# 3x3 convolutions on TensorE: minimal filtering along rows alone, against minimal filtering along rows and columns with 1 MB filter pieces

## Chip, cores, metric

One core of one Trainium2 chip, everything in float32. The metric is the device time of one execution in microseconds (us). A time given for a kernel is the median of its runs.

## The reference

Eight images of 512 channels x 32 x 32, group norm, then a block with two bottlenecks; each bottleneck has a 3x3 convolution over 256 channels followed by attention over all 1024 positions with four heads.

```python
t = cbs(x, cv1_w, cv1_bn, 0)                  # 1x1 convolution, batch norm, silu: 512 -> 512
ys = [t[:, :C], t[:, C:]]                     # C = 256
for i in range(2):
    yi = ys[-1]
    z = cbs(yi, m_cv1_w[i], m_cv1_bn[i], 1)   # the 3x3 convolution, 256 -> 256
    z = bot_attention(z, m_qkv_w[i], m_rw[i], m_rh[i])
    z = silu(bn_eval(conv2d(z, m_cv2_w[i], 0), m_cv2_bn[i]))
    ys.append(yi + z)
out = x + cbs(concatenate(ys, axis=1), cv2_w, cv2_bn, 0)
```

## The kernel before

A 3x3 convolution with output rows in tiles of four needs, for each output, fewer multiplications if rows are combined first: F(4,3) makes six combinations of six input rows, multiplies each by a combination of the filter's rows, and combines the six results into four rows. The three taps along a row remain ordinary taps. The stages are: combine filters once (first image, then kept in DRAM), combine input rows on VectorE, multiply on TensorE, combine result rows on VectorE, then silu.

```python
def make_u(n, oc, k):                          # filters, first image only
    ...
    nc.vector.tensor_tensor(even, g0, g2, ALU.add)
    nc.vector.scalar_tensor_tensor(u[:, 1], even, -4.0, odd, ALU.mult, ALU.add)
    ...                                        # 6 operations on VectorE, 3 on ScalarE
    nc.gpsimd.dma_start(u_dram[n][oc][k], u)

def conv3x3(n, vs, u_of):
    z = act.tile([P, NM, HW], F32, tag="z", name="z")
    for oc in range(NM):                       # NM = 2 blocks of 128 channels
        us = [u_of(oc, k) for k in range(NM)]
        mid = ps_big.tile([P, 4, NT * F], F32, tag="big", name="c3_mid")
        ...                                    # end: the two outer combinations
        for pos in (1, 2, 3, 4, 0, 5):         # row combinations
            dst = mid[:, pos - 1, :] if 0 < pos < 5 else end[:, pos // 5, :]
            for i in range(NM * 3):            # input block and tap
                k, dx = divmod(i, 3)
                nc.tensor.matmul(
                    dst, us[k][:, pos, dx, :], vs[k][:, pos, :, dx : dx + F],
                    start=(i == 0), stop=(i == NM * 3 - 1),
                )
        rows_out(z[:, oc, :], mid, end)        # VectorE, reads PSUM
        k = bn_m1[n] + oc
        for half in range(NH):
            part = z[:, oc, ts(half, HALF)]
            t = act.tile([P, HALF], F32, tag="t", name="t", bufs=2)
            nc.scalar.activation(t, part, AF.Tanh, scale=sh[:, k : k + 1], bias=bh[:, k : k + 1])
            nc.vector.tensor_scalar(
                part, part, sh[:, k : k + 1], bh[:, k : k + 1], ALU.mult, ALU.add
            )
            nc.vector.scalar_tensor_tensor(part, t, 1.0, part, ALU.add, ALU.mult)
    return z
```

`rows_in` (VectorE, per input block: three operations over 512 elements and six over 256) makes the row combinations `v_in`. After a convolution come the 1x1 projections to q, k and v. The first few of them need only the first block of 128 channels, and TensorE does those while the second block's output and activation are still under way. "Tail" below is the time from the start of the last convolution matmul to the first projection matmul that needs the second block.

## Time and profile before

Median 2671.78 us (2671.65 to 2671.93). The chain of waits and the groups are shown in the prediction. In the views, PE is TensorE's matmuls, PEld its weight loads, DVE VectorE, ACT ScalarE, POOL GpSimd and SP SyncE; L254 is a line of the kernel in question.

### The profile page before, as it was taken

The page shows a single profiled execution, that of the slowest core. Times are in us where ns is not written, and L with a number is a line of the kernel's source. Part 1 is how long each engine was busy: PE and PEld are TensorE (multiplying, and loading weights), DVE is VectorE, ACT ScalarE, POOL GpSimd, SP SyncE. Part 2 cuts the span into 40 slices and gives each one's busy share as a digit, 9 for nine tenths or more (in the row PEclk, how much of TensorE's full clock was granted, in tenths as well). Part 3 has the DMA queues.
Part 4 walks back from the last instruction along what each step waited for, and adds up shares of the span by engine and source line. Part 5 has one row for each costly group of instructions (what it writes and reads, how often), then busy time and mean ns, then how long its engine had stood idle before and what let it go on. Part 6 is the DMA issues. An engine that isn't in the chain of part 4 may idle for free.

```text
span 2669.4 us, 33857 instructions
## 1 busy us (share of the span) xinstructions
PE 2582.2 (97%) x13858; PEld 1300.7 (49%) x13858; DVE 1397.0 (52%) x2036; ACT 989.4 (37%) x1337; POOL 103.5 (4%) x246
## 2 busy tenths in 40 slices
PE   6999999999999999999999999999999999999898
PEld 3536355363553635446364453635536354363633
DVE  5565645645356453564636546265552645536453
ACT  2342523524234241443414434153431534315252
POOL 2000010000100001000010000100000000000000
PEclk9999999999999999999999999999999999999999
DMA  6113021030310203112031110402104011130001
GB/s 227 52 67 116 14 99 70 14 117 14 110 61 25 103 14 132 40 53 74 14 132 41 58 68 14 165 12 74 52 27 150 10 54 41 40 138 14 32 14 57
DMA packets 81571, 174.08 MB, mean 65 GB/s; under 512 B 31872, under 2 KB 41600, under 8 KB 73216
## 3 DMA queue, kind: packets, MB, share of 16 engines
q1 hardware_dynamic: 69664, 129.33, 14.2%
q0 software_dynamic: 11744, 42.51, 4.7%
q8 instruction: 111, 1.82, 0.3%
q14 instruction: 52, 0.43, 0.0%
HBM read 144.87 MB, written 26.94 MB: 64 GB/s over the span
## 4 chain that ended last, share of the span: by engine, by line
PE 86%; issue 4%; DVE 4%; ACT 3%; DMA 1%; SPq 0%; DVEq 0%; ACTq 0%
PE ps L254 33%; PE av_ps L458 14%; PE l_ps L435 13%; PE c_mid L625 12%; PE c_end L625 6%; PE v_ps L401 4%; ACT pt L439 3%; PE s_ps L475 2%; PE m_ps L647 2%; DVE acc L444 1%; DVE ao L466 1%; DVE st L325 1%; DMA rs<-r_dram 0%; DVE acc L442 0%; ACT h L240 0%
## 5 line engine op out<-in xcount | busy, mean ns | idle before, releaser
L439 ACT ACTIVATE pt<-l_ps 128x1024 f32<-128x1024 f32 x512 | 496.3, 1026 | 236.2 <-PE l_ps L435 230.4
L444 DVE TENSOR_TENSOR acc<-acc,pt 128x1024 f32<-128x1024 f32 x384 | 469.6, 1223 | 147.3 <-ACT pt L439 122.9
L458 PE MATMUL av_ps<-pt,vT 64*64 64x512 f32 x4096 | 492.9, 597 | 9.9 <-DVE ao L466 9.9
L435 PE MATMUL l_ps<-q,kr 64*64 64x512 f32 x4096 | 495.2, 599 | 2.6 <-DVE gr L344 2.2
L458 PEld LDWEIGHTS av_ps<-pt,vT 64*64 64x64 f32 x4096 | 155.7, 135 | 310.3 <-issue 232.5
L625 PE MATMUL c_mid<-v_in,u 128*128 128x256 f32 x1344 | 296.2, 379 | 8.4 <-DVE v_in L290 8.4
L435 PEld LDWEIGHTS l_ps<-q,kr 64*64 64x64 f32 x4096 | 155.3, 134 | 286.5 <-issue 268.1
L625 PEld LDWEIGHTS c_mid<-v_in,u 128*128 128x128 f32 x1344 | 254.8, 190 | 51.0 <-issue 15.4
L240 ACT ACTIVATE h<-ps,bh,sh 128x512 f32<-128x512 f32 x128 | 92.5, 773 | 406.5 <-PE ps L254 406.5
L254 PE MATMUL ps<-z,qkv_sb 128*128 128x512 f32 x512 | 229.2, 595 | 0.0
L254 PE MATMUL ps<-x,w 128*128 128x512 f32 x512 | 226.5, 599 | 2.2 <-DVE x L358 2.2
L254 PE MATMUL ps<-ypad,w 128*128 128x512 f32 x512 | 227.1, 594 | 0.0
L254 PEld LDWEIGHTS ps<-x,w 128*128 128x128 f32 x512 | 96.7, 191 | 130.0 <-issue 126.2
L254 PEld LDWEIGHTS ps<-ypad,w 128*128 128x128 f32 x512 | 96.6, 190 | 125.1 <-issue 125.1
L691 DVE SCALAR_TENSOR_TENSOR t<-t,h 128x512 f32<-128x512 f32 x64 | 41.9, 686 | 211.6 <-ACT t L241 211.6
L625 PE MATMUL c_end<-v_in,u 128*128 128x256 f32 x672 | 150.4, 379 | 0.0
L442 DVE TENSOR_TENSOR acc<-pt 128x1024 f32<-128x1024 f32 x64 | 78.4, 1225 | 137.2 <-ACT pt L439 137.2
L254 PEld LDWEIGHTS ps<-z,qkv_sb 128*128 128x128 f32 x512 | 95.9, 190 | 106.4 <-issue 95.7
L625 PEld LDWEIGHTS c_end<-v_in,u 128*128 128x128 f32 x672 | 127.6, 190 | 18.3
L304 DVE TENSOR_TENSOR sd<-c_mid,m 128x512 f32<-128x512 f32 x32 | 22.1, 691 | 212.4 <-ACT m L302 212.4
L254 PE MATMUL ps<-ylast,w 128*128 128x512 f32 x256 | 117.2, 595 | 10.5 <-DVE ylast L655 10.5
L392 DVE TENSOR_TENSOR kr<-ps,rw_sb 128x512 f32<-128x512 f32 x64 | 41.2, 686 | 160.5 <-PE ps L254 160.5
(108 smaller groups left out, 2138.6 us busy)
## 6 DMA issues: line engine op xcount, KB each, us to landing
u<-u SPq DMA_DIRECT2D x56, 1152.0 KB
w<-in_cv_w_dram SPq DMA_DIRECT2D x24, 1024.0 KB
x<-in_x_dram SPq DMA_DIRECT2D x32, 512.0 KB
x_res<-in_x_dram POOLq DMA_DIRECT2D x64, 256.0 KB, 3.9
out_dram<-t POOLq DMA_DIRECT2D x62, 256.0 KB, 3.0
rs<-r_dram SPq DMA_DIRECT2D x96, 128.0 KB
u<-u_new POOLq DMA_DIRECT2D x8, 1152.0 KB, 4.5
raw<-in_m_cv_w_dram SPq DMA_DIRECT2D x8, 576.0 KB
```

The costliest lines, as they stand in the source:

```text
L240: nc.scalar.activation(h, ps, AF.Identity, scale=sh[:, k : k + 1], bias=bh[:, k : k + 1])
L254: nc.tensor.matmul(ps[:, half, :], w_of(k), rhs_of(k, half), start=(k == 0), stop=(k == nk - 1))
L401: nc.tensor.matmul(ps[:, j, :], z[:, k, ts(j0 + j, P)], qkv_sb[:, n, k, 2 * C : 3 * C], start=(k == 0), stop=(k == NM - 1),)
L435: nc.tensor.matmul(ps[kh * HD : (kh + 1) * HD, hd, :], kr[r, c, o : o + HD], q[r, c, ts(half, HALF)], start=True, stop=True,)
L439: nc.scalar.activation(pt[:, i], ps, AF.Exp, scale=SCALE)
L442: return nc.vector.tensor_tensor(accs[g], pt[:, 0], pt[:, 1], ALU.add)
L444: ins = nc.vector.tensor_tensor(accs[g], accs[g], pt[:, i], ALU.add)
L458: nc.tensor.matmul(avs[g][hd * HD : (hd + 1) * HD, kh, :], vT[r, j, o : o + HD], pt[r, i, hd, :], start=(j == 0), stop=(j == NJ - 1),)
L475: nc.tensor.matmul(ps[hd * HD : (hd + 1) * HD, kh, :], ones[r], acc[r, hd, :], start=True, stop=True,)
L625: nc.tensor.matmul(dst, us[k][:, pos, dx, :], vs[k][:, pos, :, dx : dx + F], start=(i == 0), stop=(i == NM * 3 - 1),)
L647: nc.tensor.matmul(pss[oc][:, half, :], m2_sb[:, n, k, ts(oc, P)], ao[:, k, ts(half, HALF)], start=(k == 0), stop=(k == NM - 1),)
L691: nc.vector.scalar_tensor_tensor(t, t, 1.0, h, ALU.add, ALU.mult)
```

## The change

The intent is to multiply less. F(2,3) along columns is put on top of F(4,3) along rows: six row combinations x four column combinations replace six x three taps, but each covers only half as many columns. So a product streams 128 columns instead of 256, and there are 48 per block of 128 output channels instead of 36. A float32 product runs as two instructions (the 1152 convolution products of the kernel before are 2304 matmul instructions in its trace), so a block goes from 72 instructions of 256 columns to 96 of 128. The six row combinations are handled as three pairs, each with its own input tile, PSUM tile and 1 MB piece of filters. The price is more work on VectorE: the inputs and outputs need column transforms, and the filters too. The diff, cut to its core:

```diff
+    def make_u(n, oc, k, us, tag, raw_tag, bufs=(1, 1)):
+        ...                                   # per pair i: two row combinations "rows" as before, then
+            c0, c1, c2 = (rows[:, :, c, :] for c in range(3))
+            ends = tmp[:, 4, 0:2, :]
+            tt(ends, c0, c2, ALU.add)
+            tt(u[:, :, 1, :], ends, c1, ALU.add)
+            tt(u[:, :, 2, :], ends, c1, ALU.subtract)
+            nc.scalar.mul(u[:, :, 0, :], c0, 2.0)
+            nc.scalar.mul(u[:, :, 3, :], c2, 2.0)
...
+        def tiles_in(yp):                     # per pair and input block: rows e, then columns
+                    mid = pairs_of(1)
+                    tt(v[..., 1], mid[..., 0], mid[..., 1], ALU.add)
+                    tt(v[..., 2], mid[..., 1], mid[..., 0], ALU.subtract)
+                    tt(v[..., 0::3], pairs_of(0), pairs_of(2), ALU.subtract)
...
+        def columns_out(r, ps):
+            m2 = act.tile([P, 2, NT * NW], F32, tag="h", name="m2", bufs=2)
+            nc.scalar.copy(m2, ps[:, :, 2, :])
+            nc.vector.tensor_tensor(r[..., 0], ps[:, :, 1, :], m2, ALU.add)
+            ...                               # three more on VectorE
...
         def conv3x3(n, vs, u_of):
-                for pos in (1, 2, 3, 4, 0, 5):
-                    dst = mid[:, pos - 1, :] if 0 < pos < 5 else end[:, pos // 5, :]
-                    for i in range(NM * 3):
-                        ...
+                for i in range(PAIRS):
+                    ps = ps_big.tile([P, 2, NC, NT * NW], F32, tag="big", name="c3_ps")
+                    for row in range(2):
+                        for col in range(NC):
+                            for k in range(NM):
+                                nc.tensor.matmul(
+                                    ps[:, row, col, :], us[i][:, k, row, col, :], vs[i][:, k, row, col, :],
+                                    start=(k == 0), stop=(k == NM - 1),
+                                )
+                    columns_out(rs[i], ps)
+                    if i == 1:
+                        first()               # row outputs 1 and 2
+                last()                        # row outputs 0 and 3
                 for half in range(NH):
                     part = z[:, oc, ts(half, HALF)]
-                    t = act.tile([P, HALF], F32, tag="t", name="t", bufs=2)
-                    nc.scalar.activation(t, part, AF.Tanh, scale=sh[:, k : k + 1], bias=bh[:, k : k + 1])
-                    nc.vector.tensor_scalar(
-                        part, part, sh[:, k : k + 1], bh[:, k : k + 1], ALU.mult, ALU.add
-                    )
-                    nc.vector.scalar_tensor_tensor(part, t, 1.0, part, ALU.add, ALU.mult)
+                    silu(part, part, bn_m1[n] + oc)
```

The last lines replace "tanh straight from the part on ScalarE, scale and shift beside it on VectorE" by "scale and shift on ScalarE, then tanh on ScalarE": a longer chain with less work for VectorE.

## The prediction

The sum came to 49 + 16 - 20 = 45 us gained, and 7 more for the scheduler. The 109 ns for an instruction of 128 columns is my estimate: half of the 215.8 ns measured for 256 columns is 107.9, which would make a block 10.4 us instead of 10.5 and the removed time 166 us instead of 162. In the kernel before, "the duration here" is the 190 ns of a weight load of 128 columns, and the second load of that view starts 0.108 us after the first. The loads of 64 columns in attention came four at a time, one such group every 0.43 us. "682 to 691 and 415" are VectorE's operations on 512 and 256 float32 elements. The 0.5 us of rival (c) was supposed: no trace of the kernel before showed what an alternating write costs.

> **What bounds the kernel now.** I read the busy times and the chain that ended last, then the chain piece by piece around one convolution, then the groups of its matmuls and weight loads, then the timeline of VectorE.
>
> ```profile
> PE 2582.2 (97%) x13858; PEld 1300.7 (49%) x13858; DVE 1397.0 (52%) x2036; ACT 989.4 (37%) x1337; POOL 103.5 (4%) x246
> PE 86%; issue 4%; DVE 4%; ACT 3%; DMA 1%; SPq 0%; DVEq 0%; ACTq 0%
> L625 PE MATMUL c_mid<-v_in,u 128*128 128x256 f32 x1344 | 296.2, 379 | 8.4 <-DVE v_in L290 8.4
> L625 PEld LDWEIGHTS c_mid<-v_in,u 128*128 128x128 f32 x1344 | 254.8, 190 | 51.0 <-issue 15.4
> ```
>
> TensorE carries 86% of the chain; VectorE is half idle. The convolution waits once for its input (8.4 us, in the last image, which has no other work left to put before it).
>
> The chain at the second convolution of the second image:
>
> ```profile
> 540.35 10.36 PE c_mid L625 x48
> 550.71 5.18 PE c_end L625 x24
> 555.89 10.36 PE c_mid L625 x48
> 566.25 5.18 PE c_end L625 x24
> 571.43 3.43 PE ps L254 x8
> 574.87 0.43 PE v_ps L401 x2
> 575.30 3.63 PE ps L254 x8
> ```
>
> 48 instructions in 10.36 us are 215.8 ns each. A float32 product is two instructions (2 x 1152 matmuls in the program, 2304 in the trace over all images)[...]. A block of 128 output channels ("block") is 72 instructions = 15.54 us; there are 32 blocks (8 images, 2 convolutions, 2 blocks), so convolution is 497 us. After the last one TensorE has 3.86 us of projections that need only the first block; the second block's activation ends just as they do, so the tail after the convolution costs nothing.
>
> [...] The duration here is 190, but that isn't the rate. Two loads of 128 columns with a four-column matmul between them:
>
> ```profile
> 463.20 0.30 PEld L331 LDWEIGHTS gm_ps<-mv,gmat 128*128 128x128 f32 x2 [3.94 <-issue]
> ```
>
> They span 0.30 us, so the second starts some 0.107 us after the first[...]. [...] the trace has 682 to 691 and 415. In the timeline successive independent ones start closer together:
>
> ```profile
> 537.53 0.69 DVE L279 SCALAR_TENSOR_TENSOR w_tmp<-ypad 128x512 f32<-128x512 f32 x1
> 538.14 0.68 DVE L282 TENSOR_TENSOR w_tmp<-ypad 128x512 f32<-128x512 f32 x1
> 538.74 0.68 DVE L283 TENSOR_TENSOR w_tmp<-ypad 128x512 f32<-128x512 f32 x1
> 539.34 0.41 DVE L290 TENSOR_TENSOR v_in<-w_tmp 128x256 f32<-128x256 f32 x1
> 539.68 0.41 DVE L291 TENSOR_TENSOR v_in<-w_tmp 128x256 f32<-128x256 f32 x1
> ```
>
> So 0.605 us per 512 elements and 0.337 per 256. One that needs its predecessor's result starts some 0.03 us after its end, about 0.1 more. [...] The new writes of columns 0 and 3 alternate between far places; no access of the kernel before does, so the trace can't say.
>
> **TensorE.** Removed per block: 6 row combinations x 3 taps x 2 input blocks x 2 passes = 72 instructions of 256 columns. Added: 3 pairs x 2 rows x 4 columns x 2 input blocks x 2 passes = 96 of 128 columns. [...] I take 109: the engine already keeps one 64-column load per 107 ns in attention. Block: 96 x 0.109 = 10.5 us, 5.06 less; over 32 blocks 162 us. That is the gain if VectorE keeps up, and the rest of this is about where it doesn't.
>
> **VectorE.** Input, per pair and input block: two 512-element and four 256-element operations, two of them waiting for their predecessor: 2 x 0.605 + 4 x 0.337 + 0.2 = 2.77 us. Six of these make 16.6 us per convolution; before it was 2 x (3 x 0.605 + 6 x 0.337) = 7.7. Output per block: columns 3 x 1.45, rows 2.1 + 1.5, activation 1.2, together 9.2 us (before 5.7). This fits under 10.5 us of TensorE, but hardly. Filters, first image only: per input and output block 6 x 0.468 + 9 x 0.337 + waits = 6.6 us, before 2.9.
>
> **First convolution of images 2 to 8.** Its input is transformed during the 45 us of the preceding output convolution, where VectorE is 43% busy: hidden. The matmuls end 2 x 5.06 = 10.1 us earlier. The tail grows: copy 0.4 on ScalarE, columns 1.5, rows 1.5, then scale-and-shift of both halves 1.45, tanh 0.63, product 0.7 and hand-overs: 6.4 instead of 3.85 us, and up to 1.4 more because the copy shares two buffers with the preceding activation. Filler stays below 4 us. Gain 10.1 - 2.5 - (0 to 1.4), say 7.0; seven times 49 us.
>
> **Second convolution.** Between its input and its start lie only 13.7 us of other matmuls. In the second image VectorE begins the transform at 531.2 and, with 3.7 us of other operations between, would end it at about 551.5, where TensorE could begin at 540.3. Pair 1 is ready near 545, pair 2 at 551.5, so the first block ends at 555, as late as now. Outputs then queue: 3.0 + 2.1 + 1.5 + 1.5, activation to 562, second block to 570.5, activation to about 573. Today the dependent projection starts at 575.3. Gain 2.3; seven times 16 us. The bound moves to VectorE.
>
> **First image.** Filters cost 13.3 us per output block and lie on VectorE with everything else. First convolution: both transforms, filters and outputs fill it to some 95 us where the activation now ends at 88: 7 lost. Attention: two filter calls of 6.6 us instead of three of 2.9: 4 lost (this stretch already waits for filter work). Second convolution: 13.3 us inline instead of 2.9, less 2.3 gained: 9 lost. Sum 20 lost.
>
> **Transfers.** Filters go from 2 x 1152 KB to 3 x 1024 KB per block. In the window from 404 to 422 us the queues moved 172 GB/s x 18 us = 3.1 MB beside the matmuls without a wait; each new piece has at least one pair, 3.5 us, and for the late ones 10 us. I count nothing.
>
> Sum: 49 + 16 - 20 = 45, so 2627; I lower it to 2620 because the scheduler interleaves operations of different stages, as it does at 531 us, and may place outputs ahead of the last pair of inputs.
>
> **Rivals.** (a) *TensorE keeps the bound*, VectorE hides nearly everywhere: then about 130 of the 162 us remain, 2540 to 2560. For it: VectorE is 52% busy and would rise to about 1670 us, 63%. Against: those idle times lie in other stages. (b) *Weight loads become the bound*: if a load could not begin before its predecessor's whole 190 ns, a block takes 18 us and the kernel some 2740. For it: the 190 in the group line. Against: the 0.30 span above. At 120 ns, 2635. (c) *VectorE slower than its lines*, by strided writes: 0.5 us more on each of six operations per convolution costs 3 us in eight second convolutions, 2645. (d) *A filter transfer comes late*: three or four us per convolution would cancel half the gain; against it stands the transfer paragraph.
>
> **Range and chances.** The balance is a 162 us gain with about 115 given back by three separate stalls; each could be off by a third, so 2575 to 2665. The 2% mark is 2618, at my middle: faster 0.46, within 0.46, slower 0.08 (for (b), or (c) and (d) together).
>
> **What would show it.** Convolution matmuls starting 109 to 112 ns apart inside a pair, busy for about 340 us in all. VectorE about 1670 us busy. In second convolutions two idle times of TensorE before pairs 1 and 2 of the first block, ended by the input transform on VectorE, and none there in first convolutions. Two to four us idle ahead of the projections in each. The first image longer by about 20 us, each later image shorter by about 9. I am wrong if the matmuls are over 120 ns apart, if TensorE waits for a filter transfer, or if second convolutions gain as much as first ones.

## More of the kernel before

The span of the profiled run is 2669.4 us, with TensorE busy for 97% of it, VectorE for 52%, and a mean granted clock of 0.992. The granted clock is the share of TensorE's full clock that the throttle let through, as the profiler recorded it.

To compare the kernels stage by stage I worked out this table from the start times of TensorE's matmuls in the trace. "Convolution" is first to last convolution matmul; "projections" runs from the end of the tail to the first matmul of the logits; "rest" runs from there to the next convolution (for first convolutions a mean over images 2 to 7, since the last image has less to do there). The other columns are means over images 2 to 8 for first convolutions and 2 to 7 for second ones.

| before, us | whole stage | convolution | tail | projections | rest |
|---|---|---|---|---|---|
| first convolution, a mean image | 148.64 | 30.87 | 4.17 | 16.97 | 99.77 |
| second convolution, a mean image | 175.38 | 30.87 | 4.17 | 16.97 | 123.37 |

The start takes 53.2 us, the whole first image 335.0 (two convolutions of 30.9 in it), and from the last convolution to the end it is 188.4. Half the clock was granted for 17.1 us in all between 420 and 2460 us.

## The result

| | median us (range) | ratio to before, 95% interval | clock |
|---|---|---|---|
| before | 2671.72 (2671.53 to 2671.93) | 1 | 0.992 |
| after | 2662.26 (2658.34 to 2669.41) | 0.9968 (0.9944 to 0.9991) | 0.976 |

A ratio is the mean time of one kernel's fast runs over the mean of the other's fast runs of the same rounds, so it is not quite the ratio of the medians. The forecast was 52 us less; 9.5 us came. That is inside the range, but the gain is a fifth of the one forecast.

From the page of the kernel after (groups: busy time and mean ns of one, then idle time before them and what ended it):

```profile
PE 2469.9 (93%) x14626; PEld 1230.8 (46%) x14626; DVE 1673.7 (63%) x2780; ACT 1059.6 (40%) x1513; POOL 114.6 (4%) x378
...
L674 PE MATMUL c_ps<-v_in,u 128*128 128x128 f32 x2688 | 313.6, 280 | 37.0 <-DVE v_in L330 27.5
...
L272 PE MATMUL ps<-z,qkv_sb 128*128 128x512 f32 x512 | 245.5, 630 | 43.1 <-DVE z L264 43.1
```

The line of the kernel before that answers to the last one:

```profile
L254 PE MATMUL ps<-z,qkv_sb 128*128 128x512 f32 x512 | 229.2, 595 | 0.0
```

The engines did what was forecast: VectorE is busy 1673.7 us (forecast about 1670), TensorE 112 us less than before. But TensorE now idles 37.0 us in the convolutions (and 25.0 us more in those of the first image) and 43.1 us ahead of the projections, and the projections themselves, which nobody touched, are 16 us busier: 630 ns each instead of 595. (The chain that ended last breaks off at 2455 us in this trace and covers only the last image, so I read stages instead.)

| after, us (against before) | whole stage | convolution | tail | projections | rest |
|---|---|---|---|---|---|
| first convolution | 144.00 (-4.64) | 21.33 (-9.54) | 6.86 (+2.69) | 18.43 (+1.46) | 100.62 (+0.85) |
| second convolution | 174.88 (-0.50) | 26.66 (-4.21) | 6.87 (+2.70) | 17.98 (+1.01) | 123.38 (+0.01) |

The start takes 55.5 us (+2.3), the first image 359.7 (+24.7), the end from the last convolution on 185.7 (-2.7). The balance is 7 x (-4.64) + 6 x (-0.50) - 2.7 + 24.7 + 2.3 = -11.2 us, which is the difference of the two spans (2669.4 and 2658.2).

**The end of a first convolution.** Timeline of the kernel after, second image (start, duration, instructions; in brackets idle time before and what ended it):

```profile
436.65 3.60 PE L272 MATMUL ps<-z,qkv_sb 128*128 128x512 f32 x8
...
440.59 1.52 ACT L258 ACTIVATE h<-z,bh,sh 128x512 f32<-128x512 f32 x2 [3.32 <-DVE z L366]
442.01 1.13 ACT L259 ACTIVATE t<-h 128x512 f32<-128x512 f32 x2
442.66 1.29 DVE L264 SCALAR_TENSOR_TENSOR z<-t,h 128x512 f32<-128x512 f32 x2 [2.16 <-ACT t L259]
443.40 5.40 PE L272 MATMUL ps<-z,qkv_sb 128*128 128x512 f32 x8 [2.72 <-DVE z L264]
```

TensorE runs out of matmuls that need only the first block and waits 2.72 us for the chain row outputs, scale and shift, tanh, product. Then comes what I had not expected: eight projection matmuls of the same shape take 3.60 us before the wait and 5.40 us after it. The windows view over a stretch after that wait, and over the corresponding projections of the kernel before, says why (us, PE, PEld, DVE, ACT, POOL, granted clock, DMA share, GB/s); first the kernel after:

```profile
443.00:462.50 19.50, 19.09 (x58) 10.98 (x62) 5.93 (x10) 3.69 (x8) 0.00 (x0) 0.91 0.00 1
```

and the kernel before:

```profile
423.00:440.00 17.00, 17.00 (x56) 10.18 (x54) 6.27 (x11) 3.22 (x6) 0.00 (x0) 1.00 0.14 61
```

The granted clock falls below full: half clock for 3.4 us costs 1.7 us (0.09 x 19.5 = 1.76). All first convolutions of images 2 to 7 show it in their projections (18.67 us instead of 16.97), and of the second ones those of images 3, 5 and 7. Half clock between 420 and 2460 us grew from 17.1 to 75.1 us. Ten of its 22 stretches of 3.41 us lie in projections, four in the second convolutions of images 4 and 6 (27.4 and 27.3 us instead of 26.3), eight in the rest of first stages. Here 2.72 us of idle time were enough for half clock to follow.

Why the same wait lowered the clock in some places and not in others can be read from this trace too. Its half-clock stretches all start on one grid of 3.41 us (at 444.13 us, for instance, and 12 steps later at 485.09). The windows view by steps of that grid, around the wait of the first convolution and then that of the second, same image:

```profile
440.72:444.13 3.41, 0.72 (x2) 0.42 (x3) 1.29 (x2) 2.42 (x4) 0.00 (x0) 1.00 0.04 17
444.13:447.55 3.42, 3.42 (x5) 1.43 (x5) 1.01 (x2) 0.00 (x0) 0.00 (x0) 0.50 0.00 0
590.91:594.32 3.41, 1.57 (x5) 0.57 (x3) 1.36 (x3) 1.92 (x3) 0.00 (x0) 1.00 0.55 231
```

The first wait lies in one step, which has 2.69 us of idle time, and the next step runs at half clock. The second wait, as long, is split over two steps (1.84 us in the one shown, 0.89 in the next), and the clock stays full. From image 2 on, each of the 18 full-clock steps of this trace with at least 2.05 us idle was followed by half clock, and none of the 610 with at most 1.97 us. The line between them is that of this trace only: in the kernel before, a step with 1.91 us idle (1443.86 to 1447.27) was followed by half clock.

**A second convolution.** Timeline of TensorE, second image, kernel after. It answers to the seven pieces of the chain that the prediction shows of before:

```profile
562.02 3.96 PE L674 MATMUL c_ps<-v_in,u 128*128 128x128 f32 x34
568.83 3.84 PE L674 MATMUL c_ps<-v_in,u 128*128 128x128 f32 x32 [2.85 <-DVE v_in L330]
574.28 14.34 PE L674 MATMUL c_ps<-v_in,u 128*128 128x128 f32 x126 [1.62 <-DVE v_in L330]
...
595.21 3.70 PE L272 MATMUL ps<-z,qkv_sb 128*128 128x512 f32 x8 [2.73 <-DVE z L264]
```

The two waits before pairs 1 and 2 of the first block are those that the prediction named, ended by the input transform on VectorE, and again 2.73 us are missing ahead of the dependent projections. What VectorE did last before each pair is line 330, the write of columns 0 and 3 together. From the groups of the kernel after, with its neighbour in line 329:

```profile
L330 DVE TENSOR_TENSOR v_in<-w_rows 128x512 f32<-128x512 f32 x96 | 103.3, 1077 | 0.0
L329 DVE TENSOR_TENSOR v_in<-w_rows 128x256 f32<-128x256 f32 x96 | 41.5, 432 | 0.0
```

1077 ns for 512 elements, where the contiguous writes of the kernel before take 682 to 691: that was rival (c). The next operation starts 0.90 us after it instead of 0.605.

**The first convolution of the first image.** Timeline of TensorE, kernel after:

```profile
55.54 7.53 PE L674 MATMUL c_ps<-v_in,u_new 128*128 128x128 f32 x66
64.99 5.24 PE L674 MATMUL c_ps<-v_in,u_new 128*128 128x128 f32 x30 [1.92 <-DVE v_in L330]
77.35 0.80 PE L674 MATMUL c_ps<-v_in,u_new 128*128 128x128 f32 x2 [7.12 <-ACT u_new L229]
...
84.56 12.49 PE L674 MATMUL c_ps<-v_in,u_new 128*128 128x128 f32 x90 [2.24 <-ACT u_new L229]
```

The second block waits for its filters piece by piece: 7.12 us, then 2.24 and two shorter waits cut from the view.

### The profile page after: what moved, and what is told of

It is laid out like the page before. It is cut to its first block, busy times and chain, and to the rows that moved or that the text cites. A ratio compares the mean times of both kernels' runs of the same rounds, so it can differ in the third digit from the quotient of the medians.

```text
span 2658.2 us, 36654 instructions
## 1 busy us (share of the span) xinstructions
PE 2469.9 (93%) x14626; PEld 1230.8 (46%) x14626; DVE 1673.7 (63%) x2780; ACT 1059.6 (40%) x1513; POOL 114.6 (4%) x378
## 5 line engine op out<-in xcount | busy, mean ns | idle before, releaser
L674 PE MATMUL c_ps<-v_in,u 128*128 128x128 f32 x2688 | 313.6, 280 | 37.0 <-DVE v_in L330 27.5
L674 PEld LDWEIGHTS c_ps<-v_in,u 128*128 128x128 f32 x2688 | 310.8, 196 | 46.6 <-DVE v_in L330 30.0
L272 PE MATMUL ps<-z,qkv_sb 128*128 128x512 f32 x512 | 245.5, 630 | 43.1 <-DVE z L264 43.1
L259 ACT ACTIVATE t<-h 128x512 f32<-128x512 f32 x256 | 149.7, 622 | 32.2 <-DMA out_dram<-t 24.2
L440 DVE TENSOR_TENSOR kr<-ps,rw_sb 128x512 f32<-128x512 f32 x64 | 41.2, 686 | 186.0 <-PE ps L272 186.0
L337 ACT COPY m<-c_ps 128x256 f32<-128x256 f32 x96 | 35.8, 373 | 243.1 <-PE c_ps L674 224.2
L530 ACT COPY s_row<-s_ps 128x512 f32<-128x512 f32 x128 | 68.7, 589 | 151.2 <-PE s_ps L523 148.7
L272 PE MATMUL ps<-ylast,w 128*128 128x512 f32 x256 | 117.2, 595 | 10.5 <-DVE ylast L701 10.5
```

Of the source, the lines that this page charges most:

```text
L259: nc.scalar.activation(t, h, AF.Tanh)
L272: nc.tensor.matmul(ps[:, half, :], w_of(k), rhs_of(k, half), start=(k == 0), stop=(k == nk - 1))
L440: nc.vector.tensor_tensor(dst, img(ps[:, half, :]), rw, ALU.add)
L530: nc.scalar.copy(row, ps[:, kh, :])
L674: nc.tensor.matmul(ps[:, row, col, :], us[i][:, k, row, col, :], vs[i][:, k, row, col, :], start=(k == 0), stop=(k == NM - 1),)
```

## The experiments

My theory after the result had three parts: (1) idle time ahead of the projections costs twice, as a wait and as a lower clock; (2) the scattered write of columns 0 and 3 delays second convolutions; (3) filters cost the first image about 30 us. Rivals: the lower clock has another cause (the mere number of short matmuls), VectorE is simply too busy whatever its writes, or the first image loses its time to input and output transforms. Each edit is against the changed kernel. e1 to e4 ran together beside seven runs of before (median 2672.89), e5 to e8 likewise (2672.64).

| run | median us (range) | ratio to before, 95% |
|---|---|---|
| after | 2662.26 (2658.34 to 2669.41) | 0.9968 (0.9944 to 0.9991) |
| e1_split | 2648.38 (2646.83 to 2651.74) | 0.9908 (0.9892 to 0.9925) |
| e2_busy | 2641.78 (2639.42 to 2645.95) | 0.9888 (0.9871 to 0.9904) |
| e3_nofilter (wrong) | 2629.40 (2626.55 to 2631.32) | 0.9838 (0.9821 to 0.9854) |
| e4_act | 2624.99 (2622.55 to 2626.47) | 0.9823 (0.9807 to 0.9839) |
| e5_kr | 2609.74 (2606.51 to 2612.81) | 0.9764 (0.9748 to 0.9780) |
| e6_all | 2585.88 (2583.41 to 2586.43) | 0.9676 (0.9660 to 0.9692) |
| e7_poolf | 2592.12 (2591.91 to 2594.11) | 0.9702 (0.9686 to 0.9718) |
| e8_poolv | 2594.44 (2589.53 to 2600.18) | 0.9710 (0.9688 to 0.9731) |
| e9_load | 2640.07 (one run) | (2672.66 beside it) |

All experiments but e3 agree with the reference. Stage times of the experiments, from the traces as above (half clock from the first convolution of image 2 to that of image 8):

| us | first image | first stage: convolution, tail, projections | second stage: convolution, tail, projections | half clock, images 2 to 7 |
|---|---|---|---|---|
| before | 335.0 | 148.64: 30.87, 4.17, 16.97 | 175.38: 30.87, 4.17, 16.97 | 17.1 |
| after | 359.7 | 144.00: 21.33, 6.86, 18.43 | 174.88: 26.66, 6.87, 17.98 | 75.1 |
| e1 | 361.3 | 143.41: 21.33, 6.86, 18.43 | 173.89: 24.58, 7.28, 18.67 | 61.4 |
| e2 | 361.4 | 142.34: 21.33, 6.86, 16.97 | 173.62: 26.48, 6.86, 16.97 | 41.0 |
| e4 | 361.5 | 140.81: 21.33, 5.91, 16.97 | 172.58: 26.32, 5.97, 16.97 | 23.9 |
| e5 | 356.5 | 140.76: 21.33, 6.87, 15.26 | 172.01: 26.51, 6.86, 15.26 | 47.8 |
| e6 | 353.0 | 140.01: 21.33, 6.03, 15.26 | 169.11: 24.59, 5.97, 15.26 | 30.7 |

### e1_split: columns 0 and 3 written apart

```diff
-                    tt(v[..., 0::3], pairs_of(0), pairs_of(2), ALU.subtract)
+                    tt(v[..., 0], pairs_of(0)[..., 0], pairs_of(2)[..., 0], ALU.subtract)
+                    tt(v[..., 3], pairs_of(0)[..., 1], pairs_of(2)[..., 1], ALU.subtract)
```

> Edit: columns 0 and 3 of the transformed input are written by two operations of 256 elements, each to consecutive places, instead of one of 512 that alternates between two places 1.5 KB apart (1077 ns in the changed kernel). Theory S (the alternating write is what makes that operation slow): the two take about 430 ns each and start 0.34 apart, so 0.67 us in place of 0.96, 1.7 us less per input transform; first convolutions are unchanged (hidden), the span of matmuls in second convolutions falls from 26.3 to about 24.6 us, the first image loses 3 us less: some 15 us in all, about 2647. Rival R (the operation is slow because it has two inputs read in pairs from overlapping rows, whatever it writes): the two new ones are slow as well, 0.5 us each, and nothing is gained, about 2662.

The groups of e1 (the same elements, in two operations instead of one):

```profile
L330 DVE TENSOR_TENSOR v_in<-w_rows 128x256 f32<-128x256 f32 x96 | 40.6, 423 | 0.0
L331 DVE TENSOR_TENSOR v_in<-w_rows 128x256 f32<-128x256 f32 x96 | 40.6, 423 | 0.0
```

and its TensorE timeline in the second convolution of the second image:

```profile
567.31 3.84 PE L675 MATMUL c_ps<-v_in,u 128*128 128x128 f32 x32 [1.52 <-DVE v_in L330]
572.35 14.34 PE L675 MATMUL c_ps<-v_in,u 128*128 128x128 f32 x126 [1.20 <-DVE v_in L330]
...
593.68 5.40 PE L272 MATMUL ps<-z,qkv_sb 128*128 128x512 f32 x8 [3.13 <-DVE z L264]
```

Two operations of 423 ns replace one of 1077. Each of them reads every second element of `w_rows`, where the one operation read consecutive ones, and writes one contiguous column. So the reads are not what cost: it was the write that alternates between two columns 1.5 KB apart. (Whether the distance matters, or only that each element goes elsewhere than the one before, was not tried.) The waits shrink from 2.85 and 1.62 us to 1.52 and 1.20, and the second convolution from 26.66 to 24.58. About half of that is given back at once: the wait ahead of the projections grows to 3.13 us, and now every second convolution of images 2 to 7 shows the lower clock (18.67). The time falls by 14 us; the profiled run is the slowest of the four, so the stage table understates it.

### e2_busy: useless matmuls in the gap

The same work, and before the last row outputs six extra products of 256 columns into a free PSUM tile, which nothing reads. They remove no wait; they only keep TensorE busy.

```diff
+                if oc == NM - 1:
+                    idle = ps_av.tile([P, 2, HALF], F32, tag="av", name="idle")
+                    for _ in range(6):
+                        nc.tensor.matmul(
+                            idle[:, 0, : 2 * P], ident, r[:, 1, 0].rearrange("p q o -> p (q o)"),
+                            start=True, stop=True,
+                        )
                 last()
```

> Edit: six useless float32 products of 256 columns (12 instructions, 2.6 us) right behind the last matmul of each convolution, into the PSUM tile that is free there, so that TensorE does not stand idle while it waits for the second block's activation. Nothing that the real work waits for comes earlier. Theory C (standing idle for 2.7 us makes the granted clock fall to half for one or two stretches of 3.4 us afterwards, and this costs what the prediction lacked): the low-clock stretches some 1.5 us after the tails go, the time from the first dependent projection to the first logits returns from 18.7 to 17.0 us in all images, and the kernel gets about 1.7 us x 11 = 15 to 20 us faster although it computes more, about 2645. Rival: the slow projections come from their inputs (VectorE), not from the clock: no gain, 2660 to 2670.

TensorE's timeline in e2, second image, after the first convolution:

```profile
437.96 2.76 PE L684 MATMUL idle<-r_mid,ident 128*128 128x256 f32 x12
...
444.71 3.70 PE L272 MATMUL ps<-z,qkv_sb 128*128 128x512 f32 x8
```

and the window over the stretch that follows:

```profile
440.50:460.00 19.50, 19.37 (x63) 11.47 (x62) 6.69 (x12) 5.78 (x10) 0.00 (x0) 1.00 0.09 37
```

Nothing starts earlier: the tail is 6.86 us as in the kernel after. But the eight matmuls take 3.70 us instead of 5.40, the clock is 1.00 instead of 0.91, the projections are back at 16.97 us in both convolutions, and the kernel is 20 us faster (0.9888 against 0.9968). Work that does nothing made it faster; so the idle time itself lowered the clock, and the rival "many short matmuls lower it" falls, since those are all still there.

### e3_nofilter: no filter arithmetic (wrong result)

```diff
         for i in range(PAIRS):
-            ...                               # all row and column combinations
+            nc.scalar.mul(us[i][:, k], raw[:, 0:8].rearrange("p (r c) o -> p r c o", r=2), 1.0)
```

> Wrong result on purpose: the filters are not computed, ScalarE copies the raw weights into their places (three copies of 1024 elements per call) and VectorE does nothing for them; transfers, buffers and matmuls stay. Theory F (the first image lost 27 us because filter arithmetic on VectorE and ScalarE stands before its matmuls): the first image, from the first matmul of its first convolution to that of the next image, falls from 359.7 us to about 330, below the 335.0 of the kernel before; total about 2632. Rival T (it is the transfers of raw weights, or the ring of five buffers that a filter waits for): the first image stays above 350, total above 2650.

The output is wrong (relative error 0.149). TensorE's timeline in e3, first image:

```profile
54.20 21.60 PE L652 MATMUL c_ps<-v_in,u_new 128*128 128x128 f32 x192
...
82.38 5.40 PE L250 MATMUL ps<-z,qkv_sb 128*128 128x512 f32 x8 [2.71 <-DVE z L242]
```

All 192 matmuls run without a wait, in 21.60 us instead of 41.2. The first image takes 327.1 us: 32.6 less than after and 7.9 less than before. So the filter arithmetic is the whole loss of the first image; the rivals "input and output transforms fill it" and "transfers or the ring of buffers" fall, since those were left as they are. The lower clock ahead of the projections is there as ever (5.40), since this run did nothing about that wait.

### e4_act: the old activation

```diff
-                    silu(part, part, bn_m1[n] + oc)
+                    k = bn_m1[n] + oc
+                    t = act.tile([P, HALF], F32, tag="t", name="t", bufs=2)
+                    nc.scalar.activation(t, part, AF.Tanh, scale=sh[:, k : k + 1], bias=bh[:, k : k + 1])
+                    nc.vector.tensor_scalar(
+                        part, part, sh[:, k : k + 1], bh[:, k : k + 1], ALU.mult, ALU.add
+                    )
+                    nc.vector.scalar_tensor_tensor(part, t, 1.0, part, ALU.add, ALU.mult)
```

> Edit: the convolution's activation as in the kernel before (tanh straight from the sum with scale and bias, scaling on VectorE beside it) instead of scale-and-shift on ScalarE and then tanh. Theory: this shortens the tail from the last matmul to the first projection that needs the second block from 6.87 to about 6.1 us, at 1.1 us more VectorE work per block. First convolutions gain 0.7 us each and may fall under the idle time that makes the clock drop, another 1.7; second ones lose as much as they gain, since VectorE bounds them. About 5 us less in all, up to 15 less if the clock drops go; 2647 to 2657. Rival: VectorE has no room and the added operations cost it all: 2662 or more.

The dependent projections in e4, second image:

```profile
443.65 3.70 PE L272 MATMUL ps<-z,qkv_sb 128*128 128x512 f32 x8 [1.76 <-DVE z L690]
```

My expectation was too cautious: 37 us came. The tail is 0.95 us shorter in first convolutions and 0.90 in second ones, some 13 us over the fourteen of images 2 to 8. And with 1.76 us of idle instead of 2.72 the clock stays up (3.70 us for the eight, projections 16.97): the other 24 us, much like the 20 of e2 (half clock fell by 51 us in images 2 to 7, which is worth 26). The activation is a small part of the diff and looks like a relief for VectorE; it cost the most of all parts that could be undone alone.

### e5_kr: real work in the gap

Half of the products of one projection (k of the second 128 channels) needs only the first block of `z`. With a free PSUM tile for it, it can be issued right after the last convolution matmul.

```diff
-                    ps = conv1x1(
-                        lambda k: qkv_sb[:, n, k, o : o + P], lambda k, half: z[:, k, ts(half, HALF)], NM
-                    )
+                    early = ps_av.tile([P, NH, HALF], F32, tag="av", name="k_ps") if c * which else None
+                    parts = [range(NM)] if early is None else [range(1), range(1, NM)]
+                    for ks in parts:
+                        with tc.issue_after(marks["conv"].ins) if len(parts) > 1 else ExitStack():
+                            ps = conv1x1(
+                                lambda k: qkv_sb[:, n, k, o : o + P],
+                                lambda k, half: z[:, k, ts(half, HALF)], NM, ks, early,
+                            )
...
-                                nc.tensor.matmul(
+                                marks["conv"] = nc.tensor.matmul(
```

> Edit: the keys' projection of the second group of heads takes the PSUM tile that attention has not begun to use, so that its two products from the first block (1.7 us) can run on TensorE while it waits for the second block's activation. The filler grows from 4.0 to 5.7 us, the wait shrinks from 2.7 to about 1.0. Theory C (a long idle time lowers the clock, a short one does not): the projections take 17.0 - 1.7 us after the first dependent one in all images, both kinds of convolution gain 1.7 + 1.5 us, 15 x 3 = 45 us in all, about 2617. Rival (idle time of any length ahead of the projections costs the clock): only the 1.7 us each, 27 us in all, about 2635.

TensorE's timeline in e5, second image:

```profile
435.54 1.88 PE L274 MATMUL k_ps<-z,qkv_sb 128*128 128x512 f32 x4
...
438.42 3.70 PE L274 MATMUL ps<-z,qkv_sb 128*128 128x512 f32 x8 [1.00 <-DVE z L266]
```

The tail is unchanged (6.87), since VectorE and ScalarE set it, but 1.7 us of later work now lie inside it: projections 15.26 = 16.97 - 1.71, again without the lower clock. 2609.74 us is 52 us less than after: the 20 us of e2 and 16 x 1.7 = 27 us of moved work make up most of it.

### e6_all: e1, e4 and e5 together

> The three useful edits together: consecutive writes of the columns (e1), the activation as before (e4) and the earlier keys' projection (e5). No wait of TensorE ahead of the projections is left in first convolutions, so e4 and e5 overlap: first convolutions some 6 us shorter than in the changed kernel (tail and filler 0.95 + 1.7, clock 1.5, less than the sum where the wait is gone already), second ones 3 + 1.7 shorter. Expected 2598 to 2612, faster than both kernels. If the VectorE work added by e4 cancels e1 in second convolutions, 2612 to 2620.

```profile
433.41 1.88 PE L274 MATMUL k_ps<-z,qkv_sb 128*128 128x512 f32 x4
...
435.35 3.70 PE L274 MATMUL ps<-z,qkv_sb 128*128 128x512 f32 x8
```

In this timeline of e6, second image, no wait stands ahead of the dependent projections. Second convolutions are at 24.59 us with a tail of 5.97. 2585.88 us is 86 us (3.2%) under before and the fastest version. Against after it is 76 us less, and the three parts alone gave 14, 37 and 52: they share the recovered clock. It is also 12 us under the range that I expected.

### e7_poolf: e6, with filter columns on GpSimd

```diff
-            tt(ends, c0, c2, ALU.add)
-            tt(u[:, :, 1, :], ends, c1, ALU.add)
-            tt(u[:, :, 2, :], ends, c1, ALU.subtract)
+            gt = nc.gpsimd.tensor_tensor
+            gt(ends, c0, c2, ALU.add)
+            gt(u[:, :, 1, :], ends, c1, ALU.add)
+            gt(u[:, :, 2, :], ends, c1, ALU.subtract)
```

> e6_all, with the three column operations of each filter pair (nine of fifteen VectorE operations per call) on GpSimd, idle there. Theory F (VectorE work and its handing to and fro with ScalarE makes the first image long): 72 operations of 0.337 us leave VectorE, the first image falls by 5 to 12 us if GpSimd needs under 0.7 us for one; if it needs over 1 us the chain through GpSimd becomes longer than the one it replaces and the first image gets no shorter or up to 10 us longer. Only the first image changes.

```profile
L228 POOL TENSOR_TENSOR u_new<-u_tmp 128x256 f32<-128x256 f32 x24 | 27.4, 1141 | 2.4 <-PE ps L275 0.7
```

This group of e7 takes 1141 ns for 256 elements, and the two others of the edit 965 and 815, against some 420 on VectorE. The first image takes 362.5 us instead of 353.0, so the relief of VectorE is worth less than the slower chain. 2592.12 us.

### e8_poolv: e6, with one input column on GpSimd

```diff
-                    tt(v[..., 2], mid[..., 1], mid[..., 0], ALU.subtract)
+                    nc.gpsimd.tensor_tensor(v[..., 2], mid[..., 1], mid[..., 0], ALU.subtract)
```

> e6_all, with one of the four column operations of every input transform on GpSimd. Theory V (VectorE bounds second convolutions): six operations of 0.337 us leave it, the matmuls of second convolutions span 1 to 2 us less (toward the 21.3 of first ones), 10 to 15 us in all. Rival: GpSimd is slower at it and its result comes last, or it holds up VectorE's own two-input operations, so second convolutions get longer.

The groups of e8, GpSimd's operation and VectorE's beside it:

```profile
L331 POOL TENSOR_TENSOR v_in<-w_rows 128x256 f32<-128x256 f32 x96 | 162.1, 1690 | 323.8 <-DVE w_rows L312 273.1 <-issue 20.9 <-DVE w_rows L323 17.1
L330 DVE TENSOR_TENSOR v_in<-w_rows 128x256 f32<-128x256 f32 x96 | 61.1, 637 | 0.0
```

GpSimd takes 1690 ns, and the operation of VectorE beside it grows from 426 ns to 637. Second convolutions go from 24.59 to 26.54 us, and the time is 8.6 us above e6. The rival that was written down for this run is right. With 256 elements, a two-input operation took GpSimd two to four times as long as VectorE: 815 to 1141 ns in e7 and 1690 in e8, against 420 to 426.

### e9_load: narrow matmuls in the gap

As e2, but twelve products of 64 columns instead of six of 256.

> A measurement of one disputed cost: twelve useless float32 products of only 64 columns (24 instructions, each with a load of 128 columns of weights) behind the last matmul of each convolution. If a matmul instruction of this kind can't start sooner than its weight load allows, the 24 start about 107 to 112 ns apart, and the 111.6 ns of the convolution's 128-column matmuls are set by the load. [...] If loads and streaming exclude one another in part, between 120 and 190.

```profile
433.13 2.79 PE L684 MATMUL idle<-r_mid,ident 128*128 128x64 f32 x24
```

From this timeline of e9, 24 instructions take 2.79 us, with starts 111 to 112 ns apart, though each streams only 64 columns. The convolution's matmuls of 128 columns start 111.6 ns apart (21.33 us over 191 intervals). The same pace at half the columns means that streaming isn't what sets it: by my estimate that would have given half of 111.6, about 56 ns. The load of 128 columns of weights ahead of each is a candidate that is left; a fixed cost of each instruction would look the same here, since no run varied the width of the load, so neither is shown.

## Why the prediction missed

Forecast against measured, in us over the whole kernel:

| term of the sum | forecast | measured |
|---|---|---|
| first convolutions, images 2 to 8 | 7 x 7.0 = 49 gained | 7 x 4.64 = 32.5 gained |
| second convolutions, images 2 to 8 | 7 x 2.3 = 16 gained | 6 x 0.50 + 2.7 = 5.7 gained |
| first image and start | 20 lost | 24.7 + 2.3 = 27.0 lost |
| lowered by hand for the scheduler | 7 gained | nothing |
| sum | 52 gained | 11.2 gained (medians: 9.5) |

**Right.** That the convolution stops being TensorE's alone, and that 162 us of removed matmul time would mostly be given back. The pace: 111.6 ns lies in the 109 to 112 named. VectorE's 1670 us. The tail: forecast 2.5 to 3.9 longer, measured 2.69 and 2.70. The two waits of second convolutions and their cause; none in first ones after the first image. No wait for a filter transfer, which refutes rival (d); rival (b), loads at their full 190 ns, is refuted by the pace. Rival (a), 2540 to 2560 us, was not reached even by e6. Not as forecast: convolution matmuls are busy for 367 us and not 340, and later images are 5 us shorter and not 9.

**The step that failed: "Gain 10.1 - 2.5 - (0 to 1.4), say 7.0; seven times 49 us."** The first two terms were right (9.54 and 2.69). Missing was a term: after 2.7 us of idle, the projections run part of their time at half clock, +1.46 us in a first convolution and +1.01 in a second one, that is 7 x 1.46 + 6 x 1.01 = 16 us. e2 shows it by removing only the idleness: 20 us. I counted the wait as a wait and took the time of all that follows it from the kernel before, which never idled there. That the clock falls after a wait could have been read from that trace, in other stages: its 17.1 us of half clock. (TensorE waits 3.09 us up to 463.23 us there, for instance, and has half the clock for 3.41 us from 464.23.) Another 0.85 us per first convolution lies in the rest of the stage, and this too is clock: eight stretches of half clock there in images 2 to 7 instead of five, 3 x 1.7 / 6 = 0.85, all in images 4 and 6.

**Second term, "second convolution: gain 2.3".** The scattered write, which stood in the prediction as rival (c) at 0.5 us per operation and not in the sum, held VectorE for 0.90 us where the sum had counted 0.605 for an operation of 512 elements: 0.3 us, six times per transform. Without the clock in the projections the gain was 4.21 - 2.70 = 1.5; with it 0.50. e1 gives 2.08 us of the convolution back. That 1.5 is near 2.3 is in part luck: the forecast let the second block's matmuls wait for outputs, so that they ended 30.2 us after the first matmul (570.5 against 540.3), with the activation 2.5 us behind them. In the trace they run without a wait, 26.3 us in all, and the tail takes 6.87.

**Third term, the first image.** Attention (4 forecast, 3.8 measured) and second convolution (9 forecast, though its terms 13.3 - 2.9 - 2.3 make 8.1; 8.1 measured) were right. "First convolution: 7 lost" was 10.4 in the convolution and 2.4 in the tail. The two calls for filters stretched over 19.8 us (72.05 to 91.88) instead of 13.3: VectorE stood idle for 4.0 us of it, in the longest pieces for ScalarE, and spent about 3 on outputs between, which a sum of filter durations doesn't hold. After the waits the clock was low here as well (0.81 granted from 84.5 to 97.0 us): the 30 and the 90 matmuls of the view above took about 4 us more than at the pace of 111.6 ns. e3 shows that filters are behind all of the loss; how it divides between the waits and the clock is read from the trace alone.

**The last correction**, 7 us more gain for the scheduler's interleaving, had no measurement behind it and was wrong in full.

**What stays open.** A wait of 2.7 us lowers the clock or not by where it falls on the grid of 3.41 us (in the kernel after, the projections show it behind 9 of the 16 convolutions; the second ones of images 2, 4, 6 and 8, for instance, escaped), and waits of 1.76 us stay below what was seen to do it (1.91 us in one step of the kernel before, 2.05 in the kernel after). The grid lies elsewhere in the two traces (its steps begin 0.01 us after a multiple of 3.41 us from the span's start in the kernel before, 0.40 us in the kernel after), so a single run's count of low stretches is in part chance. Half clock for 31 us remains in images 2 to 7 even in e6. Whether filters could be combined without delaying the first image, other than by GpSimd, I did not try.

## What to carry to other kernels

When a change cuts matmul time, look for the places where TensorE will now run dry, and count an idle stretch of about 2 us or more twice (1.91 us in one step of the grid was the least seen here to be followed by half clock): the wait, and the slower work that may follow it (1.7 us for each 3.41 us at half clock). Filling it with real work that has its inputs already (half a projection into a free PSUM tile) was worth more than any of the other repairs (52 us in e5), and even useless matmuls paid (20 us in e2). When outputs are to go to several places, one strided write that alternates between them can cost more than two plain ones (here 1077 ns against 2 x 423).
